# First tokens' norm and first gate/up product inside layer 0's last attention group; a written order behind layer 1's last attention unit

## The chip, the cores and the metric

The kernel runs on one core of one Trainium2 chip. A NeuronCore has five engines that run side by side, each with its own in-order queue: TensorE (PE in the profile) multiplies matrices and also transposes 128x128 blocks against an identity; VectorE (DVE) and ScalarE (ACT) do element-wise work and read results out of PSUM; GpSimd (POOL) does element-wise work in SBUF and issues DMAs; SyncE (SP) issues DMAs. The metric is device time in microseconds (us), lower is better. The kernel before was timed three times.

## The reference

Two transformer blocks are applied to 1024 tokens of width 512, all in float32. Each block is modulated by a condition vector (six columns of `silu(c) @ wmod`: two shifts, two scales and two gates):

```python
h = layernorm(x) * (1 + ca) + sa
x = x + ga * attention(h)
h = layernorm(x) * (1 + cb) + sb
x = x + gb * ffn(h)
```

In layer 0, attention has 32 query heads and 8 key/value heads of width 128 with rotary positions and a causal mask; its weights are 4-bit integers with group scales. Its FFN is `silu(gate(x)) * up(x)` through `down`, hidden width 1376, each of the three matrices with a rank-16 addition. In layer 1, attention has 32 query heads and 8 key/value heads of width 16, with biases. Its FFN is one base matrix, `xf @ base_W.T`, plus a mixture of 28 rank-8 experts, of which the two with the highest logits count, weighted by a softmax over the two.

## The kernel before

The 1024 tokens are eight tiles `x[0]` to `x[7]` of 128 tokens, kept in SBUF. "Half 0" is tiles 0 to 3 and half 1 is tiles 4 to 7. A layer norm works per tile (`bn_stats`, `bn_aggr` on DVE, a square root on ACT, a reciprocal and the scaled copy `xn` on DVE); then a half's four `xn` tiles are transposed chunk by chunk (16 PE transposes of 128x128), and the four chunks are evicted with shift and scale, two by DVE and two by ACT, to `hT`, the transposed input that all products read.

**Layer 0's attention** runs over eight groups (`g`), one for each key/value head with its four query heads, and within a group over eight query tiles in the order 3, 7, 2, 6, 1, 5, 0, 4 (`Step`). A step computes scores, the exponential, the transposition of the probabilities (on DVE, then by DMAs), `context` (probabilities times values, copied by ACT to `ctxT`), `project_o` and `residual`, which multiplies by the gate on DVE and adds to `x[qi]`, before on POOL. Contexts and projections run two to three steps behind the scores. In the last group (`last_group_step`) token tile after token tile becomes final in `x`. The tail behind the loop handles the steps for tiles 5, 0 and 4 (`steps[-3:]`). This whole stage stands under `manual_schedule`: each engine issues the stage's instructions in the order of the program. Outside of such regions a planner orders the instructions of each engine; it may also place later, free instructions among those of a written region.

**Layer 0's FFN** is free. `ln_half` norms and transposes both halves. `merge_gate_up` and `merge_down` add the rank-16 products to the loaded weights (a small matmul into PSUM, then a DVE addition into `gu` or `dwt`). For each of eleven hidden chunks `j` and both halves `b` there are 2x4 matmuls of 128x512 for gate and up, a sigmoid on ACT and two DVE products into `hid`. The weights of chunk 0 (`fw["gu"]`) are loaded and merged during the last attention group; the other chunks' loads go out on SP (`gu`) and POOL (`dwt`) once layer 0's attention frees the memory. `bank()` hands out the seven PSUM banks of the ring.

**Layer 1's attention** runs over sixteen units (`Unit`: query half `Q`, key/value head `g`). Context products run two steps behind; `later` and `tick` keep these due. `normalize` turns a unit's context, divides by the row sums and stores it by four DMAs into `cT`. After the last unit of a query half, `finish` enqueues `project_out` for that half's four tiles, whose result is added to `x` on POOL. From unit 13 on, the order is the planner's.

**Layer 1's FFN**: for half 0 the norm, the products with expert inputs and logits (`ffn1_logits`) and the choice of experts (`ffn1_route`, a chain of some twenty small DVE operations and one ACT exponential) run beside units 13 and 14. `ffn1_turn` weights one tile's expert inputs (`hg`) and transposes them (two PE transposes, two ACT copies to `hgT`); `ffn1_out` makes the base product (4 chunks) and the two expert products in one PSUM bank, applies the gate, adds `x` and stores the tile. Behind the last unit the program has, in this order: the four `ffn1_turn` of half 0, half 1's `project_out`, half 1's norm and transposes, four `ffn1_out` of half 0, then for half 1 the logits, the routing and, tile by tile, `ffn1_turn` and `ffn1_out`.

Of the kernel before, what the change touches and what calls it, by code (L numbers as in the profile page):

```python
# [17 lines left out]
P = 128  # L18
S = 1024
NT = S // P  # L20
D = 512
# [21 lines left out]
def block_kernel(ctx: ExitStack, tc: tile.TileContext, a: dict, out: bass.AP):  # L43
# [120 lines left out]

    keep = ctx.enter_context(tc.tile_pool(name="keep", bufs=1))


    with ExitStack() as st:
# [194 lines left out]

        def residual(u, ps):
            t = tmp("ot")
            nc.vector.tensor_mul(t, ps, mod[0, 2])  # L366
            nc.gpsimd.tensor_tensor(x[u.qi], x[u.qi], t, ALU.add)  # L367

# [229 lines left out]
        for g in range(NKV):  # L598
            for i, qi in enumerate((3, 7, 2, 6, 1, 5, 0, 4)):
# [56 lines left out]
                if old:  # L656
                    residual(old, ps)
        residual(steps[-3], project_o(steps[-3]))
        for old in steps[-2:]:
            context(old)  # L660
            residual(old, project_o(old))

# [4 lines left out]
    big = st.enter_context(tc.tile_pool(name="big", bufs=1))  # L667
    hTc = {}

# [4 lines left out]
    def bank():  # L674
        return sp.tile([P, 512], F32, tag="sc", name="sc")

    xns = {}

# [17 lines left out]
    def ln_turn(half, shift, scale1, chunks=range(NC)):  # L696

        if 0 in chunks:
            hTc[half] = keep.tile([P, NC, 512], F32, tag=f"h{half}", name=f"hT{half}")
        h = hTc[half]  # L700
        for c in chunks:
            ps = bank()
            for i in range(4):
                nc.tensor.transpose(
                    ps[:, bass.ts(i, P)], xns[4 * half + i][:, bass.ts(c, P)], ident
                )
            if c % 2:
                nc.scalar.activation(
                    h[:, c, :], ps, AF.Identity,
                    bias=shift[:, c : c + 1], scale=scale1[:, c : c + 1],  # L710
                )
            else:
                nc.vector.tensor_scalar(
                    h[:, c, :], ps, scale1[:, c : c + 1], shift[:, c : c + 1],
                    ALU.mult, ALU.add,
                )

# [12 lines left out]
    with ExitStack() as f0:  # L730
# [17 lines left out]
        for j in range(NF):  # L748
            nc.gpsimd.dma_start(dwt[:, j, :], a["d_w"][bass.ts(j, P), :])

# [25 lines left out]

        for half in range(2):
            ln_half(half, mod[0, 3], mod[0, 4])

        for pair in range(2):  # L780
            merge_gate_up(1, pair)
        gate_row(0, 5, bank)

        for b in range(2):
            hid[b] = big.tile([P, NF, 512], F32, tag=f"b{b}", name=f"hid{b}")
        for j in range(NF):
            w = gu[:, j] if j else fw["gu"]
            for b in range(2):
                pgu = []
                for m in range(2):  # L790
                    ps = bank()
                    for c in range(NC):
                        nc.tensor.matmul(  # L793
                            ps, lhsT=w[:, m, c, :], rhs=hTc[b][:, c, :],
                            start=(c == 0), stop=(c == NC - 1),
                        )
                    pgu.append(ps)
                sg = wk.tile([P, 512], F32, tag="sg", name="sg")
                nc.scalar.activation(sg, pgu[0], AF.Sigmoid)
                nc.vector.tensor_mul(sg, pgu[0], sg)  # L800
                nc.vector.tensor_mul(hid[b][:, j, :], pgu[1], sg)
            if j in (0, 1, 4, 5):
                merge_gate_up(4 if j < 4 else 8, j % 4)
            elif j in (6, 7, 8):
                for i in range(4 * (j - 6), min(NF, 4 * (j - 5))):
                    merge_down(i)
# [309 lines left out]
    def project_out(t):  # L1116
# [7 lines left out]
        nc.vector.tensor_mul(o, po, mod[1, 2])  # L1124
        nc.gpsimd.tensor_tensor(x[t], x[t], o, ALU.add)

# [82 lines left out]
    def ffn1_turn(t):  # L1209
        lp = late_pool["p"]  # L1210
        hg = lp.tile([P, NE, ER], F32, tag="hg", name="hg")
        nc.vector.tensor_tensor(
# [13 lines left out]

    def ffn1_out(t):
        hgT, eb = late_pool["hgT", t], late_pool["eb"]
        po = bank()
        for c in range(NC):  # L1230
            nc.tensor.matmul(  # L1231
                po, lhsT=tok(c, t), rhs=late_pool["wb"][:, c, :], start=(c == 0), stop=False
            )
        nc.tensor.matmul(po, lhsT=hgT[:, 0, :], rhs=eb[0], start=False, stop=False)
        nc.tensor.matmul(po, lhsT=hgT[: NER - P, 1, :], rhs=eb[1], start=False, stop=True)
        o = tmp("eo")
        nc.vector.tensor_mul(o, po, mod[1, 5])
        nc.vector.tensor_add(o, o, x[t])
        nc.sync.dma_start(out[bass.ts(t, P), :], o)


# [13 lines left out]
    def finish(u):  # L1255
        normalize(u)
        if u.g == NKV - 1:
            for i in range(4):
                later(3 + i, lambda t=4 * u.Q + i: project_out(t))

# [37 lines left out]
    for n, u in enumerate(units):  # L1298
# [29 lines left out]
        while beside and beside[0][0] <= n:  # L1328
            beside.pop(0)[1]()
    for i in range(4):  # L1330
        tick()
        ffn1_turn(i)
    while late:
        tick()
    ln_half(1, mod[1, 3], mod[1, 4])
    for i in range(4):
        ffn1_out(i)
    ffn1_logits(1)
    ffn1_route()
    for t in range(4, NT):  # L1340
        ffn1_turn(t)
        ffn1_out(t)

# [83 lines left out]
```

## Time and profile before

| what | value |
|---|---|
| median of 3 runs | 1906.38 us (1901.47 to 1908.9) |
| the profiled execution's own time | 1906.41 us |
| span in its profile (first to last instruction) | 1903.7 us |
| TensorE (PE) busy | 1816.8 us, 95% of the span |
| VectorE (DVE) busy | 1162.4 us, 61% |
| ScalarE (ACT) busy | 670.2 us, 35% |
| GpSimd (POOL) busy | 483.3 us, 25% |
| mean granted TensorE clock | 0.976 |
| PE busy from 1064.00 to 1118.40 us (end of layer 0's attention to the first gate/up product) | 44.77 of 54.40 us |
| PE busy from 1838.00 to 1899.30 us (half 1's transposes to the last product) | 55.53 of 61.30 us |

The profile is one execution; its times are counted from the start of its span. In a row of the timeline stand the start and the time in us, engine, line of the kernel, operation, output and inputs, shape, the number of instructions and, in brackets, the idle time before it and what ended that. A 128x512 float32 product is recorded as two matmuls. A row of the waits has: who waited for whom, us in total, how often, the longest. "Granted clock" is the share of the full clock that TensorE's throttle let through.

### The profile page before, as it was taken

The page shows a single profiled execution, that of the slowest core. Times are in us where ns is not written, and L with a number is a line of the kernel's source. Part 1 is how long each engine was busy: PE and PEld are TensorE (multiplying, and loading weights), DVE is VectorE, ACT ScalarE, POOL GpSimd, SP SyncE. Part 2 cuts the span into 40 slices and gives each one's busy share as a digit, 9 for nine tenths or more (in the row PEclk, how much of TensorE's full clock was granted, in tenths as well). Part 3 has the DMA queues.
Part 4 walks back from the last instruction along what each step waited for, and adds up shares of the span by engine and source line. Part 5 has one row for each costly group of instructions (what it writes and reads, how often), then busy time and mean ns, then how long its engine had stood idle before and what let it go on. Part 6 is the DMA issues. An engine that isn't in the chain of part 4 may idle for free.

```text
span 1903.7 us, 22550 instructions
## 1 busy us (share of the span) xinstructions
PE 1816.8 (95%) x6578; PEld 847.0 (44%) x6578; DVE 1162.4 (61%) x2820; ACT 670.2 (35%) x1393; POOL 483.3 (25%) x717
## 2 busy tenths in 40 slices
PE   7989999999999999999999989998998989999987
PEld 4444455444454444454444444444543433333434
DVE  5677775777756777756767652323555567677332
ACT  1143433444334344334345410010123433455620
POOL 1234443444424444434444410001001000000010
PEclk9999999999999999999999999999989979999999
DMA  6164552454534544524545450010000011000000
GB/s 224 47 171 119 132 144 73 117 140 125 138 83 108 136 117 122 150 74 108 146 119 142 113 212 1 0 37 14 1 2 8 8 42 37 4 8 8 4 18 33
DMA packets 87034, 156.38 MB, mean 82 GB/s; under 512 B 25264, under 2 KB 33072, under 8 KB 86912
## 3 DMA queue, kind: packets, MB, share of 16 engines
q1 hardware_dynamic: 68480, 114.11, 21.1%
q0 software_dynamic: 18192, 40.42, 8.6%
q8 instruction: 53, 0.87, 0.2%
q14 instruction: 69, 0.57, 0.1%
q10 hardware_dynamic: 240, 0.41, 0.1%
HBM read 74.90 MB, written 2.36 MB: 41 GB/s over the span
## 4 chain that ended last, share of the span: by engine, by line
PE 71%; DVE 15%; issue 5%; ACT 5%; DMA 2%; POOL 1%; SPq 1%; ACTq 0%; POOLq 0%; DVEq 0%
PE mm L347 9%; PE sc L793 8%; PE sc L312 8%; PE mm L200 7%; PE mm L358 7%; PE sc L1043 6%; PE sc L996 5%; PE sc L812 4%; PE ctx L1086 4%; DVE pr L336 3%; PE mm L280 3%; PE sc L893 3%; ACT pr L322 2%; ACT pr L331 2%; PE sc L1231 2%
## 5 line engine op out<-in xcount | busy, mean ns | idle before, releaser
L322 ACT ACTIVATE pr<-sc,nb 128x512 f32<-128x512 f32 (+7 forms) x256 | 189.1, 739 | 508.6 <-DVE nb L320 391.1
L200 PE MATMUL mm<-hT,wf 128*128 128x512 f32 x640 | 294.3, 604 | 10.2 <-DVE t L209 7.3
L338 POOL DMA_DIRECT2D pT<-pr x509 | 251.1, 499 | 146.9 <-DMA pT<-pr 43.1
L312 PE MATMUL sc<-kT,qT 128*128 128x512 f32 (+15 forms) x768 | 263.7, 467 | 3.8 <-ACT pr L322 3.0
L347 PE MATMUL mm<-pT,v 128*128 128x512 f32 x576 | 258.8, 594 | 2.8 <-DVE gu L566 1.6
L336 DVE STREAM_TRANSPOSE pr<-pr 128x512 f32<-128x512 f32 (+7 forms) x256 | 189.2, 760 | 82.4 <-ACT pr L331 78.2
L358 PE MATMUL mm<-wo,ctxT 128*128 128x512 f32 x512 | 230.8, 593 | 3.9 <-ACT ctxT L353 2.8
L1043 PE MATMUL sc<-q,kv 32*128 32x512 f32 (+3 forms) x768 | 214.0, 557 | 8.4 <-DVE mx L1006 8.4
L312 PEld LDWEIGHTS sc<-kT,qT 128*128 128x128 f32 x768 | 141.9, 190 | 159.8 <-issue 144.5
L331 ACT ACTIVATE pr<-pr,rs 128x512 f32<-128x512 f32 (+7 forms) x256 | 190.8, 765 | 8.3 <-DVE rs L329 8.3
L1059 ACT ACTIVATE pspace<-sc 128x512 f32<-128x512 f32 (+3 forms) x303 | 132.1, 495 | 163.4 <-PE sc L1052 125.3
L200 PEld LDWEIGHTS mm<-hT,wf 128*128 128x128 f32 x640 | 120.1, 193 | 149.2 <-issue 122.8
L320 DVE TENSOR_REDUCE nb<-sc 128x1 f32<-128x416 f32 (+31 forms) x256 | 181.1, 707 | 8.8
L996 PE MATMUL sc<-kv,q 32*128 32x512 f32 (+3 forms) x768 | 172.1, 547 | 3.3 <-ACT kv L947 1.4
L367 POOL TENSOR_TENSOR x<-x,ot 128x512 f32<-128x512 f32 x64 | 81.0, 1266 | 349.7 <-DVE ot L366 273.6
L347 PEld LDWEIGHTS mm<-pT,v 128*128 128x128 f32 x576 | 107.6, 190 | 122.2 <-issue 113.0
L1006 DVE CUSTOM_DVE_ANT_0 q<-sc,cwide 128x512 f32<-128x512 f32 (+3 forms) x256 | 125.4, 490 | 56.5 <-PE sc L996 27.2
L793 PE MATMUL sc<-hT,gu 128*128 128x512 f32 x352 | 153.1, 594 | 0.0
L358 PEld LDWEIGHTS mm<-wo,ctxT 128*128 128x128 f32 x512 | 95.9, 190 | 111.4 <-issue 100.9
L1043 PEld LDWEIGHTS sc<-q,kv 32*128 32x128 f32 x768 | 78.0, 192 | 96.6 <-ACT pspace L1059 32.6
L213 POOL TENSOR_TENSOR qT<-t,t 128x512 f32<-128x512 f32 x64 | 86.8, 1356 | 112.1 <-DVE t L209 111.7
L793 PEld LDWEIGHTS sc<-hT,gu 128*128 128x128 f32 x352 | 66.2, 190 | 85.2 <-issue 80.4
(188 smaller groups left out, 1845.6 us busy)
## 6 DMA issues: line engine op xcount, KB each, us to landing
wm<-in_wmodT_dram SPq DMA_DIRECT2D x44, 256.0 KB
wi<-in_qw_q_dram SPq DMA_DIRECT2D x32, 256.0 KB
ws<-in_s_q_dram SPq DMA_DIRECT2D x32, 256.0 KB
wi<-in_qw_o_dram SPq DMA_DIRECT2D x32, 256.0 KB
ws<-in_s_o_dram SPq DMA_DIRECT2D x32, 256.0 KB
pT<-pr SPq DMA_DIRECT2D x64, 128.0 KB
pT<-pr POOLq DMA_DIRECT2D x64, 128.0 KB, 3.2
pT<-pr SPq DMA_DIRECT2D x64, 112.0 KB
```

Source lines behind the costliest of these rows:

```text
L200: nc.tensor.matmul(ps, lhsT=wf[:, c, :], rhs=hT[half][:, c, :], start=(c == 0), stop=(c == NC - 1),)
L312: nc.tensor.matmul(ps[:, n0 : n0 + w], lhsT=q, rhs=kT[u.g][:, n0 : n0 + w], start=True, stop=True)
L320: nc.vector.tensor_reduce(nb, ps[:, : d0 + B], AX.X, ALU.max, negate=True)
L322: nc.scalar.activation(u.pr[:, :, :, s, :].rearrange("p j k i -> p k j i"), ps[:, :nk].rearrange("p (k j i) -> p k j i", j=NB, i=B), AF.Ex ...
L331: nc.scalar.activation(pr, pr, AF.Copy, scale=u.rs[s])
L336: nc.vector.transpose(t, t)
L338: queues[(REP * b + r) % len(queues)].dma_start(u.pT[b * B : (b + 1) * B, r, :, :, :].rearrange("p k s i -> p (k s i)"), t[r * B : (r + 1) ...
L347: nc.tensor.matmul(ps, lhsT=vv[u.g][:, kj, :], rhs=u.pT[:, :, kj, :, :], start=(kj == 0), stop=(kj == u.n - 1),)
L358: nc.tensor.matmul(ps, lhsT=u.ctxT[:, r, :], rhs=wo[u.g][:, r, :], start=(r == 0), stop=(r == REP - 1),)
L793: nc.tensor.matmul(ps, lhsT=w[:, m, c, :], rhs=hTc[b][:, c, :], start=(c == 0), stop=(c == NC - 1),)
L996: nc.tensor.matmul(ps[:, at : at + w], lhsT=u.q[kp, bass.ts(i, P)], rhs=kT1[kp, u.g, n0 : n0 + w], start=True, stop=True,)
L1043: nc.tensor.matmul(ps[:, : QW - q0], lhsT=kT1[kp, u.g, bass.ts(kb, P)], rhs=u.q[kp, q0:QW], start=True, stop=kb < 4 * u.Q,)
```

## The change

Three things are rearranged; the arithmetic stays as it is but for which engine does some additions.

1. In the tail of layer 0's attention, inside the written region, tiles 3, 2 and 1 and then 0 are normed (`ffn_norm`, its `xn` in weight buffers of the attention that are free by then), and half 0's 16 transposes and four evictions stand between `context` and `project_o` of the last step (tile 4). The additions into `x[0]` and `x[4]` move from POOL to DVE.
2. In layer 0's FFN the first gate/up product (chunk 0, half 0) comes first, ahead of half 1's norm (tiles 7, 6, 5, then 4), its transposes and the merges of chunks 1 to 3. The eleven `dwt` loads move from POOL's queue to SP's, behind the `gu` loads.
3. Behind layer 1's last unit all engines follow a written order. Half 1's `project_out` is no longer due from `finish`; it stands behind the first two `ffn1_out`, each tile followed by its norm, with the addition into `x` on DVE. The other two `ffn1_out` stand before and behind half 1's transposes. `ffn1_out` is split into `ffn1_base` and `ffn1_experts`, and in half 1 the letters give the order: b for base, t for turn, e for experts. `hg` gets a second buffer, and each `ffn1_turn` of half 0 stands before a `tick` instead of behind it.

```diff
@@ -163,6 +163,21 @@
     keep = ctx.enter_context(tc.tile_pool(name="keep", bufs=1))
+
+    hTc, xns = {}, {}
+
+    def ln_evict_chunk(h, ps, c, shift, scale1):
+
+        if c % 2:
+            nc.scalar.activation(
+                h[:, c, :], ps, AF.Identity,
+                bias=shift[:, c : c + 1], scale=scale1[:, c : c + 1],
+            )
+        else:
+            nc.vector.tensor_scalar(
+                h[:, c, :], ps, scale1[:, c : c + 1], shift[:, c : c + 1],
+                ALU.mult, ALU.add,
+            )
     with ExitStack() as st:
@@ -361,10 +376,10 @@
                 )
             return ps
-        def residual(u, ps):
+        def residual(u, ps, eng=nc.gpsimd):
             t = tmp("ot")
             nc.vector.tensor_mul(t, ps, mod[0, 2])
-            nc.gpsimd.tensor_tensor(x[u.qi], x[u.qi], t, ALU.add)
+            eng.tensor_tensor(x[u.qi], x[u.qi], t, ALU.add)
         def plan(g, i):
@@ -655,17 +670,46 @@
                     turn_probs(u, b, queues)
                 if old:
                     residual(old, ps)
+
+
+        def ffn_norm(ts, tag, bufs):
+            mv = small.tile([P, 4, 2], F32, tag="mv", name="mv")[:, : len(ts), :]
+            for i, t in enumerate(ts):
+                bs = small.tile([P, 6], F32, tag="bnst", name="bnst")
+                nc.vector.bn_stats(bs, x[t])
+                nc.vector.bn_aggr(mv[:, i, :], bs)
+            rstd = small.tile([P, 4], F32, tag="rstd", name="rstd")[:, : len(ts)]
+            nc.scalar.activation(rstd, mv[:, :, 1], AF.Sqrt, bias=eps_t)
+            nc.vector.reciprocal(rstd, rstd)
+            for i, t in enumerate(ts):
+                xns[t] = wp.tile([P, D], F32, tag=tag, name="xn", bufs=bufs)
+                nc.vector.tensor_scalar(
+                    xns[t], x[t], mv[:, i, 0:1], rstd[:, i : i + 1], ALU.subtract, ALU.mult
+                )
+
         residual(steps[-3], project_o(steps[-3]))
-        for old in steps[-2:]:
-            context(old)
-            residual(old, project_o(old))
+        context(steps[-2])
+        ffn_norm([3, 2, 1], "wi", 3)
+        residual(steps[-2], project_o(steps[-2]), nc.vector)
+        ffn_norm([0], "wf", 2)
+        context(steps[-1])
+        hTc[0] = keep.tile([P, NC, 512], F32, tag="h0", name="hT0")
+        for c0 in range(0, NC, 2):
+            ps = sp.tile([P, 2, 512], F32, tag="sc", name="sc")
+            for c in range(c0, c0 + 2):
+                for t in range(4):
+                    nc.tensor.transpose(
+                        ps[:, c - c0, bass.ts(t, P)], xns[t][:, bass.ts(c, P)], ident
+                    )
+            for c in range(c0, c0 + 2):
+                ln_evict_chunk(hTc[0], ps[:, c - c0, :], c, mod[0, 3], mod[0, 4])
+        residual(steps[-1], project_o(steps[-1]), nc.vector)
     st = ctx.enter_context(ExitStack())
     big = st.enter_context(tc.tile_pool(name="big", bufs=1))
-    hTc = {}
     sp = st.enter_context(tc.tile_pool(name="ring", bufs=7, space=PSUM))
@@ -673,8 +717,6 @@
     def bank():
         return sp.tile([P, 512], F32, tag="sc", name="sc")
-
-    xns = {}
     def ln_tiles(ts):
@@ -704,16 +746,7 @@
                 nc.tensor.transpose(
                     ps[:, bass.ts(i, P)], xns[4 * half + i][:, bass.ts(c, P)], ident
                 )
-            if c % 2:
-                nc.scalar.activation(
-                    h[:, c, :], ps, AF.Identity,
-                    bias=shift[:, c : c + 1], scale=scale1[:, c : c + 1],
-                )
-            else:
-                nc.vector.tensor_scalar(
-                    h[:, c, :], ps, scale1[:, c : c + 1], shift[:, c : c + 1],
-                    ALU.mult, ALU.add,
-                )
+            ln_evict_chunk(h, ps, c, shift, scale1)
     def ln_half(half, shift, scale1):
         ln_tiles(range(4 * half, 4 * half + 4))
@@ -746,7 +779,7 @@
         for j in range(4, NF):
             nc.sync.dma_start(gu[:, j, :, :, :], a["gu_w"][j])
         for j in range(NF):
-            nc.gpsimd.dma_start(dwt[:, j, :], a["d_w"][bass.ts(j, P), :])
+            nc.sync.dma_start(dwt[:, j, :], a["d_w"][bass.ts(j, P), :])
         def merge_gate_up(j0, pair):
@@ -774,31 +807,37 @@
             )
             nc.vector.tensor_tensor(dwt[:, j, :], dwt[:, j, :], ps, ALU.add)
-        for half in range(2):
-            ln_half(half, mod[0, 3], mod[0, 4])
-
+        for b in range(2):
+            hid[b] = big.tile([P, NF, 512], F32, tag=f"b{b}", name=f"hid{b}")
+
+        def gate_up(j, b):
+            w = gu[:, j] if j else fw["gu"]
+            pgu = []
+            for m in range(2):
+                ps = bank()
+                for c in range(NC):
+                    nc.tensor.matmul(
+                        ps, lhsT=w[:, m, c, :], rhs=hTc[b][:, c, :],
+                        start=(c == 0), stop=(c == NC - 1),
+                    )
+                pgu.append(ps)
+            sg = wk.tile([P, 512], F32, tag="sg", name="sg")
+            nc.scalar.activation(sg, pgu[0], AF.Sigmoid)
+            nc.vector.tensor_mul(sg, pgu[0], sg)
+            nc.vector.tensor_mul(hid[b][:, j, :], pgu[1], sg)
+
+
+        gate_up(0, 0)
+        ln_tiles([7, 6, 5])
+        ln_tiles([4])
+        ln_turn(1, mod[0, 3], mod[0, 4])
         for pair in range(2):
             merge_gate_up(1, pair)
         gate_row(0, 5, bank)
-
-        for b in range(2):
-            hid[b] = big.tile([P, NF, 512], F32, tag=f"b{b}", name=f"hid{b}")
         for j in range(NF):
-            w = gu[:, j] if j else fw["gu"]
             for b in range(2):
-                pgu = []
-                for m in range(2):
-                    ps = bank()
-                    for c in range(NC):
-                        nc.tensor.matmul(
-                            ps, lhsT=w[:, m, c, :], rhs=hTc[b][:, c, :],
-                            start=(c == 0), stop=(c == NC - 1),
-                        )
-                    pgu.append(ps)
-                sg = wk.tile([P, 512], F32, tag="sg", name="sg")
-                nc.scalar.activation(sg, pgu[0], AF.Sigmoid)
-                nc.vector.tensor_mul(sg, pgu[0], sg)
-                nc.vector.tensor_mul(hid[b][:, j, :], pgu[1], sg)
+                if (j, b) != (0, 0):
+                    gate_up(j, b)
             if j in (0, 1, 4, 5):
                 merge_gate_up(4 if j < 4 else 8, j % 4)
             elif j in (6, 7, 8):
@@ -1122,7 +1161,7 @@
             )
         o = tmp("ao")
         nc.vector.tensor_mul(o, po, mod[1, 2])
-        nc.gpsimd.tensor_tensor(x[t], x[t], o, ALU.add)
+        (nc.gpsimd if t < 4 else nc.vector).tensor_tensor(x[t], x[t], o, ALU.add)
     late_pool = {}
@@ -1208,7 +1247,7 @@
     def ffn1_turn(t):
         lp = late_pool["p"]
-        hg = lp.tile([P, NE, ER], F32, tag="hg", name="hg")
+        hg = lp.tile([P, NE, ER], F32, tag="hg", name="hg", bufs=2)
         nc.vector.tensor_tensor(
             hg,
             late_pool["ha"][:, t % 4, :NER].rearrange("p (e r) -> p e r", r=ER),
@@ -1224,13 +1263,16 @@
         nc.scalar.copy(hgT[: NER - P, 1, :], ps[: NER - P, P : 2 * P])
         late_pool["hgT", t] = hgT
-    def ffn1_out(t):
-        hgT, eb = late_pool["hgT", t], late_pool["eb"]
+    def ffn1_base(t):
         po = bank()
         for c in range(NC):
             nc.tensor.matmul(
                 po, lhsT=tok(c, t), rhs=late_pool["wb"][:, c, :], start=(c == 0), stop=False
             )
+        late_pool["po", t] = po
+
+    def ffn1_experts(t):
+        hgT, eb, po = late_pool["hgT", t], late_pool["eb"], late_pool["po", t]
         nc.tensor.matmul(po, lhsT=hgT[:, 0, :], rhs=eb[0], start=False, stop=False)
         nc.tensor.matmul(po, lhsT=hgT[: NER - P, 1, :], rhs=eb[1], start=False, stop=True)
         o = tmp("eo")
@@ -1238,6 +1280,10 @@
         nc.vector.tensor_add(o, o, x[t])
         nc.sync.dma_start(out[bass.ts(t, P), :], o)
+    def ffn1_out(t):
+        ffn1_base(t)
+        ffn1_experts(t)
+
     late = []
@@ -1255,8 +1301,8 @@
     def finish(u):
         normalize(u)
         if u.g == NKV - 1:
-            for i in range(4):
-                later(3 + i, lambda t=4 * u.Q + i: project_out(t))
+            for i in range(4 if u.Q == 0 else 0):
+                later(3 + i, lambda t=i: project_out(t))
@@ -1327,19 +1373,28 @@
             open_late()
         while beside and beside[0][0] <= n:
             beside.pop(0)[1]()
+
+
+    end = ExitStack()
+    end.enter_context(tc.manual_schedule())
     for i in range(4):
+        ffn1_turn(i)
         tick()
-        ffn1_turn(i)
     while late:
         tick()
-    ln_half(1, mod[1, 3], mod[1, 4])
-    for i in range(4):
-        ffn1_out(i)
+    for t in (0, 1):
+        ffn1_out(t)
+    for t in range(4, NT):
+        project_out(t)
+        ln_tiles([t])
+    ffn1_out(2)
+    ln_turn(1, mod[1, 3], mod[1, 4])
+    ffn1_out(3)
     ffn1_logits(1)
     ffn1_route()
-    for t in range(4, NT):
-        ffn1_turn(t)
-        ffn1_out(t)
+    for step in "b4 b5 t4 b6 t5 e4 b7 t6 e5 t7 e6 e7".split():
+        {"b": ffn1_base, "t": ffn1_turn, "e": ffn1_experts}[step[0]](int(step[1]))
+    end.close()
 def _layouts(v):
```

## The prediction

> **What bounds the kernel now.** I read the page first: PE is busy 95% of the span and PE carries 71% of the chain that ended last, so time can only come out of PE's own gaps. Then the waits of PE in the two stretches that the change touches (1010 to 1120 us and 1780 to 1904 us):
>
> ```profile
> PE sc L704 <- DVE xn L692: 5.2, 1, 5.2
> ...
> PE sc L1220 <- DVE hg L1212: 6.6, 3, 5.6
> PE sc L704 <- DVE xn L692: 4.4, 1, 4.4
> ```
>
> The transposes (L704) wait for half 1's norm in layer 0's FFN, again in layer 1's, and the turns (L1220) for the routing. PE's timeline at the first place shows what the wait costs on both sides:
>
> ```profile
> 1094.04 4.53 PE L347 MATMUL mm<-pT,v 128*128 128x512 f32 x10
> 1100.00 3.70 PE L358 MATMUL mm<-wo,ctxT 128*128 128x512 f32 x8 [1.43 <-ACT ctxT L353]
> 1104.48 1.96 PE L704 MATMUL sc<-ident,xn 128*128 128x128 f32 x16 [0.79 <-DVE ot L366]
> 1111.67 3.76 PE L704 MATMUL sc<-ident,xn 128*128 128x128 f32 x16 [5.22 <-DVE xn L692]
> 1115.36 2.46 PE L760 MATMUL sc<-lB,lA 16*128 16x384 f32 x16
> ...
> 1118.25 7.03 PE L793 MATMUL sc<-hT,gu 128*128 128x512 f32 x16
> ```
>
> The same 16 transposes take 1.96 us before the idle 5.22 us and 3.76 behind it. The windows tell why: the granted clock is 0.50 from 1111 to 1115 and is back near 1115.5. PE's timeline at the end:
>
> ```profile
> 1817.13 0.43 PE L1086 MATMUL ctx<-pspace,kv 128*32 128x128 f32 x8
> ...
> 1819.80 13.90 PE L1119 MATMUL sc<-wo,cT 128*128 128x512 f32 x32
> 1838.08 3.67 PE L704 MATMUL sc<-ident,xn 128*128 128x128 f32 x16 [4.38 <-DVE xn L692]
> ...
> 1862.60 6.96 PE L1165 MATMUL sc<-wag,hT 128*128 128x252 f32 x32
> 1875.20 0.48 PE L1220 MATMUL sc<-ident,hg 128*128 128x128 f32 x1 [5.64 <-DVE hg L1212]
> ...
> 1875.68 5.74 PE L1231 MATMUL sc<-wb,hT 128*128 128x512 f32 x8
> ...
> 1898.24 1.02 PE L1235 MATMUL sc<-eb,hgT 96*128 96x512 f32 x2
> ```
>
> Two idle gaps, each followed by slow work: transposes at 3.67 instead of 1.96, a base product at 5.74 instead of the 3.60 of the others.
>
> **Change at layer 0's FFN.** Count from the end of the last context, 1098.6, which stays where it is. Is half 0's last norm in time for it? `ctxT` of tile 0 is copied by 1090.4 as before. DVE multiplies tile 5's residual until 1089.7, then norms tiles 3, 2, 1: three statistics at 0.66 with the aggregate, to 1091.7; the square root's table load (1.28) runs 1090.4 to 1091.7 on ACT as before; square root and reciprocal to 1092.4; three `xn` at 0.57 to 1094.1. Tile 0's product ends at 1094.2, as before, so its residual is not delayed: multiply 0.73, add on DVE 0.7 (nearest row: the SBUF addition L1238, 0.69; POOL took 1.27), statistics 0.85, square root 0.35, reciprocal 0.25, `xn` 0.6: ready at 1097.7, 0.9 before PE asks. That square root is now ahead of the `ctxT` copy without waiting, where before the copy stood behind a square root that waited for DVE: the 1.43 us go.
>
> PE then: 16 transposes 1.96 to 1100.6 (cover for the `ctxT` copy, 0.6); `project_o` 3.6 to 1104.1; the ring's first bank still waits for the residual's multiplication (L366), 0.8, to 1104.9; the first gate/up product 6.95 (half of L793's 13.9) to 1111.9. Under it DVE adds `x[4]` (1105.6) and norms it, 2.2, to 1107.8, or 1109.5 if the other three `xn` come first; with a table load for the square root 1110.8: still covered. Transposes at full clock 1.96, merges 2.46, gate transposes 0.6: 1116.9. Before, the same point with one product less was 1118.25. Saved: 1118.25 - (1116.9 - 6.95) = **8.3 us**. From there PE is full until layer 1's preparation, so it stays saved.
>
> At nothing: the `dwt` loads on SP. SP alone moved 371 to 411 GB/s when it loaded `lA`, `lB`, `dA`, `dB` (1099 to 1104), as much as both queues together behind it (397 to 408). Queued behind `gu` on SP, 2.9 MB of `dwt` come last (8.1 MB at 400 GB/s: 20 us), and the first merge into them stands behind chunk 6, seven times 13.9 = 97 us on. `gu` 1 to 3 come sooner than before; without that cover the merges would wait, at most the 7 us in which 2.9 MB pass.
>
> **Change at the end.** Up to the last context (ends 1817.56) nothing changes. In the written order the last `hg` stands on DVE behind `normalize` of the last unit, and the last turn stands on PE ahead of the first base product. So PE waits: context copy on ACT to 1818.3, DVE from 1818.47, `normalize` undisturbed 2.2 (unit 14's rows, 1805.15 to 1807.35), `hg` 0.4, turn 0.3: the first `ffn1_out` starts at 1821.4, with PE idle for some 3.2 us from about 1817.9. Before, `project_out` started at 1819.8. Queued behind that waiting turn is all of PE's rest, and nothing else waits.
>
> From 1821.4 only work that exists now: four `ffn1_out` at 5.15 (1847.14 to 1852.29 and so on) 20.6; `project_out` 13.8; transposes 1.96; logits 6.86; half 1's four tiles at 5.375 (1883.19 to 1888.57) 21.5. Sum 64.7, end at 1886.1 against 1899.26: **13.2 us**. What hides what:
> - `normalize`'s stores are behind 10.3 us of `ffn1_out`.
> - Norms: per tile multiply 0.73, add 0.73, statistics and aggregate 0.9, square root 0.33, reciprocal 0.2, `xn` 0.58, 3.5 us against PE's 3.44. The last `xn` is ready at 1835.2 + 14.0 = 1849.2; the transposes come behind the third `ffn1_out`, at 1850.6. At 4.2 per tile PE would wait 1.4.
> - The evictions lie under the fourth `ffn1_out` (5.15).
> - Routing: from the last logits to the turn now 5.64 + 0.5; two base products give 6.88. Without that cover it costs the 5.6 us plus 2.5 of slow clock of today.
> - The third routed tile's turn and the rest interleave products of 1.7 to 3.4 us with `hg` (0.4) and copies (0.5).
>
> **The clock behind the new gap.** The trace has no gap of 3.2 us. Its nearest rows:
>
> ```profile
> 994.40 4.14 PE L312 MATMUL sc<-kT,qT 128*128 128x512 f32 x6 [2.98 <-ACT pr L322]
> ...
> 1319.69 0.69 PE L704 MATMUL sc<-ident,xn 128*128 128x128 f32 x4 [2.25 <-DVE xn L692]
> 1320.97 8.40 PE L893 MATMUL sc<-wqkv,hT 128*128 128x512 f32 x16 [0.59 <-issue]
> 1332.35 1.10 PE L946 MATMUL sc<-ident,qpad 128*128 128x128 f32 x8 [2.98 <-DVE qpad L919]
> ```
>
> The first was followed by a granted clock of 0.50 from 996 to 999.3 (half of 3.3 us lost, 1.65), the second by 0.50 from 1320 to 1326 (8.40 where the same products later take 5.4, 3.0 lost), the third by 1.00. The longer gaps of 4.38 and 5.64 lost 2.1 and 2.5. Ends 0 and 3.0; I take 1.65, from the row whose gap and neighbours are nearest. The end is then worth 11.5. The Trainium skill ("TensorE: Matmul & The Clock Gate", "HAM oscillation — how this bites in real kernels") states that gaps up to about 3.4 us do no harm; by that rule the term is 0 and the time 1885.0, but the row at 991.4 disagrees.
>
> Sum: 1906.4 - 8.3 - 11.5 = **1886.6**. The profiled execution (1906.41, span plus 2.7) equals the median of 1906.38, so nothing is converted.
>
> **Rivals.**
> - *Norms behind the product.* If the planner queues tiles 7 to 4's norms on DVE behind the first product's own multiplications, they start at 1112.6: three statistics, square root and `xn` 4.5, tile 4's 2.2, transposes at 1119.3 instead of 1111.9, plus 1.8 of slow clock. Layer 0 then loses 0.9 (7.4 + 1.8 - 8.3) and the time is 1895.8. For: program order. Against: in this trace the planner put free statistics (1096.32) ahead of the written multiplication at 1103.73.
> - *Transposes count as idle for the clock.* Behind the first product come 5.0 us of transposes, 16-row merges and transposes. If they let the clock fall, the next product loses what the row at 1320.97 lost, 3.0: 1889.6. For: that row, where 1.5 us of transposes stand ahead of the gap. Against: behind the 5.22 us gap the clock came back during the transposes themselves. The Trainium skill (same page, "Part 4: PE-mode transpose") states that transposes do not count as busy; the row at 1320.97 fits that, those 3.8 us from 1111.67 to 1115.5 contradict it.
> - *No change or slower.* Units 13 to 15 are planned freely and the region behind them is now chained. If the planner then puts context products ahead of exponentials that ACT has not done, PE waits at each as at 1805.17 (0.82). There are 24 key blocks, each with two bunches of products. One wait per block costs 19.7: 1906.3. Two per block cost 39.4: 1926. It ends over 0.5% slower from 1.2 us a block. For: ACT is 93% busy at 1776 to 1786. Against: the contexts run two blocks behind, and before the change only two such waits stand in the trace (1.6 in all).
> - *The change doesn't order what it says*, if something of the region is held by a buffer (six `tmp` slots, of which four hold `xn`): one stored tile's chain, 1.4 us of DVE plus some 3 to land, per wait: 1891.
>
> **Numbers.** Forecast 0.70; norms behind the product 0.07; transposes as idle 0.10; buffers 0.05; no change 0.04, slower 0.04. The range takes in no clock loss (1885.0), the ring's bank free at once (0.8 less) and planner luck of 2 to 3 us below, 1881; above, the clock at 3.0, a late last norm, and the norm rival, 1896. About 0.5% (9.5 us) is what a measurement of this kernel can tell from no change: faster means under 1896.9, slower over 1915.9. Forecast and the first three small rivals are faster (0.92), less 0.04 for two of them together: faster 0.88, same 0.08, slower 0.04.
>
> **What would show it.** Right: no L692 wait of PE over 1 us left at either place; the product's 16 matmuls (now `gate_up`) directly behind the last `project_o`; one gap of about 3 us before the first base product, the only one until the end; granted clock 1.00 from the routing on. Wrong: transposes of half 1 in layer 0 starting over 2 us behind the first product; PE waiting for `hg` behind the second base product; context waits in units 13 to 15 summing to over 5 us.

## The result: 22 us faster, and the profile after

The changed kernel takes 1884.56 us (median of 4 runs, 1882.88 to 1886.94) against 1906.99 us (4 runs, 1901.47 to 1908.9). The ratio is 0.9888 with a 95% interval from 0.9865 to 0.9911. The forecast was 1886.6 us with a range from 1881 to 1896. The profiled execution of the changed kernel took 1886.94 us, with a span of 1885.1. It is the slowest of its four runs, so the two spans differ by 18.6 us and the medians by 22.4. Only one execution below, the profiled one of experiment 2's first run, was of another kind (2642.33 us at a mean granted clock of 0.69), and no comparison uses it.

PE's timeline at the end of layer 0's attention, to be held against the one before (columns as there):

```profile
1095.07 4.45 PE L362 MATMUL mm<-pT,v 128*128 128x512 f32 x10
1099.46 1.94 PE L701 MATMUL sc<-ident,xn 128*128 128x128 f32 x16
1101.23 3.60 PE L373 MATMUL mm<-wo,ctxT 128*128 128x512 f32 x8
1105.71 7.10 PE L819 MATMUL sc<-hT,gu 128*128 128x512 f32 x16 [0.88 <-DVE ot L381]
1112.65 1.91 PE L746 MATMUL sc<-ident,xn 128*128 128x128 f32 x16
1114.49 2.46 PE L793 MATMUL sc<-lB,lA 16*128 16x384 f32 x16
1116.89 0.66 PE L154 MATMUL sc<-ident,spread 128*128 128x128 f32 x4
1117.38 7.03 PE L819 MATMUL sc<-hT,gu 128*128 128x512 f32 x16
```

The gap of 5.22 us is gone, and with it the slow transposes: both sets take 1.9 us. The one wait left is for the ring's first bank. The stage now starts a microsecond later in the span (1099.52 for 1098.57), so it is measured from the end of the last context.

PE's timeline at the end of the kernel:

```profile
1808.09 0.43 PE L1125 MATMUL ctx<-pspace,kv 128*32 128x128 f32 x8
...
1811.81 0.33 PE L1259 MATMUL sc<-ident,hg 128*128 128x128 f32 x1 [2.93 <-DVE hg L1251]
...
1812.09 3.60 PE L1269 MATMUL sc<-wb,hT 128*128 128x512 f32 x8
...
1841.28 1.91 PE L746 MATMUL sc<-ident,xn 128*128 128x128 f32 x16
...
1854.98 7.03 PE L1269 MATMUL sc<-wb,hT 128*128 128x512 f32 x16
1861.85 0.27 PE L1259 MATMUL sc<-ident,hg 128*128 128x128 f32 x1
...
1874.80 0.33 PE L1259 MATMUL sc<-ident,hg 128*128 128x128 f32 x1 [1.81 <-DVE hg L1251]
...
1875.07 1.90 PE L1276 MATMUL sc<-eb,hgT 128*128 128x512 f32 x2
1876.77 1.88 PE L1277 MATMUL sc<-eb,hgT 96*128 96x512 f32 x2
```

The waits of 4.38 us for the norm and 5.64 us for the routing are gone: the transposes at 1841.28 and the first routed turn at 1861.85 start without any. The first gap was forecast (3.2 us, it is 2.93). The second, 1.81 us with expert products at 1.90 instead of 1.02 behind it, was not.

Where the 18.6 us come from, by stretches of PE's timeline (ends of the records; "net" is less 6.95 us for the product that is already done):

| stretch | before | after | difference |
|---|---|---|---|
| A: end of layer 0's last context to the first product behind the gate transposes, net | 19.68 | 10.91 | -8.77 |
| middle: from there to layer 1's last context, with the 6.95 us | 699.31 | 698.09 | -1.22 |
| B: end of layer 1's last context to the last product | 81.70 | 71.85 | -9.85 |
| start of the span to A, and the last stores | 1103.01 | 1104.25 | +1.24 |

### The profile page after: what moved, and what is told of

Read it like the earlier page. It is cut to its first block, busy times and chain, and to the rows that moved or that the text cites. A ratio compares the mean times of both kernels' runs of the same rounds, so it can differ in the third digit from the quotient of the medians.

```text
span 1885.1 us, 22551 instructions
## 1 busy us (share of the span) xinstructions
PE 1810.6 (96%) x6578; PEld 844.4 (45%) x6578; DVE 1169.5 (62%) x2831; ACT 671.7 (36%) x1398; POOL 469.5 (25%) x700
## 4 chain that ended last, share of the span: by engine, by line
PE 72%; DVE 15%; ACT 5%; issue 4%; DMA 2%; SPq 1%; POOL 1%; ACTq 0%; DVEq 0%; POOLq 0%
PE mm L362 10%; PE sc L819 8%; PE sc L327 8%; PE mm L215 7%; PE mm L373 7%; PE sc L1082 6%; PE sc L1035 5%; PE sc L851 4%; PE ctx L1125 4%; DVE pr L351 3%; PE mm L295 3%; PE sc L932 3%; ACT pr L337 2%; ACT pr L346 2%; DVE t L224 2%
```

## The experiments

Each run gives A and B from its own profile in the same way; that separates terms of 2 us, which the total times, 4 to 7 us apart between runs of one kernel, can't. Where no number of runs is given, it is one execution. The kernel before was timed beside them again: its median was 1906.75 us beside experiments 1 to 4 (9 runs, 1901.95 to 1908.42) and 1900.63 beside experiments 9 to 11 and the second run of experiment 2 (7 runs, 1898.73 to 1906.63).

**1. Only the layer 0 part.** The end is as before, the rest as in the changed kernel.

```diff
-    end.enter_context(tc.manual_schedule())
-    for i in range(4):
-        ffn1_turn(i)
-        tick()
...
+    for i in range(4):
+        tick()
+        ffn1_turn(i)
...
```

> Only the layer 0 part of the change; the end stays as before. Theory (the two parts are independent, each saves only what lies in its own stretch): from the end of the last context of layer 0's attention to the first product behind the gate transposes, 17.9 us with one product (6.95) already inside, that is 10.9 net against 19.7 before; the end stretch, from the last context to the last product, stays at 81.7. Time 8.8 below before: about 1898. Rival (the parts lean on each other, or the planner lays the free stages between them differently): the stretch between them changes by over 2 us, and the time lies outside 1895 to 1901.

Measured: A 10.90, B 81.66, and 1895.84 us (6 runs), ratio 0.9949 [0.9935, 0.9964]. A and B are what they are in the changed kernel and in the kernel before, so the parts are independent. The middle was 694.0 instead of 698 or 699, over 2 us away, which the rival had named as one of its two signs; the last section shows that this is the clock's.

**2. Only the end.** Layer 0 as before. It ran twice: the first run gives the time, the second the stretches.

```diff
-        residual(steps[-2], project_o(steps[-2]), nc.vector)
-        ffn_norm([0], "wf", 2)
...
+        for old in steps[-2:]:
+            context(old)
+            residual(old, project_o(old))
```

> Only the end of the change (written order, split products, additions on DVE); layer 0 as before. Theory: end stretch 71.9 us as in the changed kernel, with PE's two gaps of 2.9 and 1.8 us, layer 0 stretch 19.7 as before; time 9.9 below before, about 1897. Rival (the end gains part of its 9.9 us only because everything arrives earlier or in another memory layout): end stretch over 74 us.

> Only the end of the change, once more, for its stretches: the profiled execution of the second experiment ran at a mean granted clock of 0.69. Theory: end stretch 71.9 us, or 70.1 where the clock does not fall behind the gap of 1.8 us; layer 0 stretch 19.7. Rival: end stretch over 74 us.

Measured: 1898.27 us, ratio 0.9955 [0.9937, 0.9973] over three executions; in the second run A 19.77 and B 73.55. That second run took 1900.65 us in all, no less than the kernel before beside it (1900.63), although its B is 8.2 us shorter than that of the kernel before (81.70): its middle, 700.0 us, is the longest of all. B lies between what the two theories named: it is 1.7 above the changed kernel's 71.85. PE's timeline of that run shows the same two gaps, and slow products behind both:

```profile
1823.70 0.33 PE L1220 MATMUL sc<-ident,hg 128*128 128x128 f32 x1 [2.93 <-DVE hg L1212]
...
1823.97 5.29 PE L1230 MATMUL sc<-wb,hT 128*128 128x512 f32 x8
...
1888.38 0.33 PE L1220 MATMUL sc<-ident,hg 128*128 128x128 f32 x1 [1.81 <-DVE hg L1212]
...
1889.94 1.91 PE L1238 MATMUL sc<-eb,hgT 96*128 96x512 f32 x2
```

The product at 1823.97 took 5.29 where the changed kernel's took 3.60: 1.69 us, the whole difference. So the clock term that the prediction put behind the first gap exists, but it fell out in one execution and not in the other.

**3. The two turns moved.** Half 0's last turn ahead of the last unit's `normalize`, tile 7's ahead of tile 5's experts.

```diff
     for i in range(4):
         ffn1_turn(i)
-        tick()
+        if i != 2:
+            tick()
...
-    for step in "b4 b5 t4 b6 t5 e4 b7 t6 e5 t7 e6 e7".split():
+    for step in "b4 b5 t4 b6 t5 e4 b7 t6 t7 e5 e6 e7".split():
```

> The changed kernel with two moves in the written order: the last turn of half 0 ahead of the last unit's normalize, and the turn of tile 7 ahead of the experts of tile 5. Theory (both gaps of PE in the end come from DVE's own queue: a weighting that could run is queued behind operations that wait): the gap of 2.9 us goes, the gap of 1.8 us goes and with it the half clock behind it (1.7 us); end stretch 71.9 - 3.1 - 3.5 = 65.2 us, time about 1878. Rival (the next thing is late in their place: the base product waits for the copies of the turns, or the last experts for the copy of tile 7's turn, or the clock falls anyway): end stretch 68 us or more.

Measured: B 64.97, 1875.72 us (4 runs, 1872.33 to 1877.89), ratio to before 0.9839 [0.9822, 0.9857]. Both gaps are gone; no wait of PE is left in B:

```profile
1800.74 0.33 PE L1259 MATMUL sc<-ident,hg 128*128 128x128 f32 x1
...
1801.02 0.27 PE L1259 MATMUL sc<-ident,hg 128*128 128x128 f32 x1
...
1801.24 3.60 PE L1269 MATMUL sc<-wb,hT 128*128 128x512 f32 x8
...
1860.25 0.27 PE L1259 MATMUL sc<-ident,hg 128*128 128x128 f32 x1
...
1860.47 1.02 PE L1276 MATMUL sc<-eb,hgT 128*128 128x512 f32 x2
```

Its median is the lowest of this study; by B, experiments 5 and 9 are its equals.

**4. The first product back at its old place.** Half 0's early norm stays.

```diff
-        gate_up(0, 0)
         ln_tiles([7, 6, 5])
```

> The changed kernel with the first gate/up product back at its old place behind the gate transposes; half 0's early norm and transposes stay. Theory (the product is the cover for tile 4's norm): PE waits about 3.6 us from the last projection to the last xn of half 1, the transposes behind that gap run at half clock (1.8 us more); layer 0 stretch 15.4 us net against 10.9, so the early norm alone is worth 4.3 of the 8.8 us and the product's place 4.5. Without a clock drop 13.6. Rival (the early norm does it all, and the cover is not needed because the planner fills the wait with merges): 10.9 to 11.5.

Measured: A 15.35.

```profile
1101.18 3.60 PE L373 MATMUL mm<-wo,ctxT 128*128 128x512 f32 x8
1108.43 2.93 PE L746 MATMUL sc<-ident,xn 128*128 128x128 f32 x16 [3.66 <-DVE xn L734]
```

PE waits 3.66 us for tile 4's norm, and the transposes and merges behind are slow. So 4.4 of the 8.8 us hang on the product as a cover (wait and clock).

**5. The end without the written region.** Same program order, planned by the scheduler.

```diff
-    end.enter_context(tc.manual_schedule())
```

> The changed kernel without the written region at the end: the same program order, but the planner orders each engine. Theory (the gain of the end is in the split products and the program order, and both gaps are made by the written queues): the planner puts the weightings where they can run, both gaps go, end stretch 65 to 68 us against 71.9. Rival (the written order carries the gain): the planner lets the base products of half 1 start late or packs the routing without cover, and the end stretch is 75 us or more.

Measured: B 64.98, in one execution of 1877.76 us. DVE's timeline shows what the planner does otherwise:

```profile
1804.98 0.39 DVE L1251 TENSOR_TENSOR hg<-ha,oh 128x224 f32<-128x224 f32 x1 [9.45 <-PE sc L1260]
1805.92 0.39 DVE L1251 TENSOR_TENSOR hg<-ha,oh 128x224 f32<-128x224 f32 x1 [0.55 <-PE sc L1260]
1807.00 0.71 DVE L1141 STREAM_TRANSPOSE q<-q 128x512 f32<-128x512 f32 x1 [0.69 <-ACT q L1134]
```

Both `hg` (the lines with L1251) stand ahead of `normalize` (L1141). In the changed kernel the second of them stands behind it:

```profile
1810.77 0.71 DVE L1148 STREAM_TRANSPOSE q<-q 128x512 f32<-128x512 f32 x1
1811.40 0.35 DVE L1251 TENSOR_TENSOR hg<-ha,oh 128x224 f32<-128x224 f32 x1
```

The gain of the end thus needs no written region: it lies in what this version keeps, the split products, the additions on DVE, the second `hg` buffer and the program order, which no run takes apart. The written region as it was changed gave 6.9 us of it back, and a planned order ends where that of experiment 3 does.

**6. Only tile 7's turn moved.**

> The changed kernel with only the turn of tile 7 moved ahead of the experts of tile 5. Theory: the second gap (1.8 us) and the slow experts behind it (1.7 us) go, the first gap of 2.9 us stays without a clock drop: end stretch 68.4 us. Rival (the half clock is owed to the first gap or to the moment, not to the second gap): the experts of tiles 6 and 7 still take 1.9 us a piece, 70 us.

Measured: B 68.12; the experts behind take 1.02, the gap of 2.93 stays, with a base product of 3.60 behind it. Together with experiment 3, the first gap is worth 68.12 - 64.97 = 3.15 us, the second 71.85 - 68.12 = 3.73.

**7. The `dwt` loads back on POOL's queue.**

```diff
-            nc.sync.dma_start(dwt[:, j, :], a["d_w"][bass.ts(j, P), :])
+            nc.gpsimd.dma_start(dwt[:, j, :], a["d_w"][bass.ts(j, P), :])
```

> The changed kernel with the down weights' loads back on POOL's queue. Theory: nothing moves, as the first merges have their weights in time either way: layer 0 stretch 10.9 us net, plus or minus 0.3. Rival (two queues share the DMA engines, and the gate and up weights of chunks 1 to 3 then come too late for the merges, which now stand earlier): DVE waits for loads ahead of its first merge, up to 7 us.

Measured: A 13.12, so the rival was right. DVE's timeline:

```profile
1117.08 3.80 DVE L798 TENSOR_TENSOR gu<-gu,sc 128x384 f32<-128x384 f32 x8 [2.67 <-DMA gu<-in_gu_w_dram]
```

The first merge waits 2.67 us for the `gu` loads, and PE 1.9 us behind it for a bank. The DMA engines are full (a share of 1.01 to 1.03 from 1108 to 1118), and with both queues at work they carry `dwt` beside `gu`. In the kernel before the first merge (1116.31) waited for no load. This queue move looks like a detail and is 2.2 of the 8.8 us. It is worth more than A shows: behind PE's wait the granted clock is 0.50 from 1119.7 to 1123.1, and the first product of the middle takes 8.73 us where the changed kernel's takes 7.03.

**8. Half 1's projections ahead of the first two output tiles.**

```diff
-    for t in (0, 1):
-        ffn1_out(t)
     for t in range(4, NT):
         project_out(t)
         ln_tiles([t])
+    for t in (0, 1):
+        ffn1_out(t)
```

> The changed kernel with half 1's projections ahead of the first two output tiles of half 0. Theory: the stores of the last unit are the only thing that the two tiles covered; they are issued from about 1811.5 on this trace's clock and are needed 2.6 us behind the first product (the last chunk of tile 4), so PE waits 0 to 1.5 us; the norms get more cover, not less: end stretch 71.9 to 73.4 us. Rival (the stores land late, 4 us or more, as with loads of that queue): PE waits over 3 us there and the clock falls: 76 us.

Measured: B 70.98, below what either theory named. PE stood still for 0.58 us ahead of the seventh projection matmul. The profile names no releaser for it ("issue"), but experiment 10 waits for the stores at the same place, and in both that matmul starts 6.89 us behind the last context. The second gap, however, passed without a fall of the clock:

```profile
1872.13 0.33 PE L1259 MATMUL sc<-ident,hg 128*128 128x128 f32 x1 [1.81 <-DVE hg L1251]
...
1872.41 1.02 PE L1276 MATMUL sc<-eb,hgT 128*128 128x512 f32 x2
```

The same 1.81 us, between the same instructions as in the changed kernel, and experts at 1.02 instead of 1.90.

**9. Another PSUM bank for the last projection**, on top of experiment 3.

```diff
-        residual(steps[-1], project_o(steps[-1]), nc.vector)
+        ps = sp.tile([P, 2, 512], F32, tag="sc", name="sc")[:, 0, :]
...
+        residual(steps[-1], ps, nc.vector)
```

> The two moves of the third experiment, and the last projection of layer 0's attention writes into a score bank, so that the ring's first bank, which the first gate/up product takes, no longer waits for the last residual's multiplication. Theory: PE's wait of 0.9 us ahead of that product goes: layer 0 stretch 10.0 us net against 10.9; end stretch 65.0 as in the third experiment; time about 1875. Rival (the ring waits for the whole old pool, whichever bank was read last): 10.9 again.

Measured: A 10.91, with the wait of 0.88 for the residual's multiplication as before; B 64.98; 1877.43 us (4 runs), ratio 0.9872 [0.9846, 0.9898] to the 1900.63 us beside it. The bank that was read last is not the reason, or not by itself. Whether the ring waits for the whole old pool or happens to begin at the new bank stays open.

**10. Projections first, with the turns moved** (experiments 3 and 8 together).

> The two moves of the third experiment, and half 1's projections ahead of the first two output tiles. Theory (the first two output tiles cover the last unit's stores once the gap ahead of them is closed): the stores were usable 6.9 us behind the last context with the gap; without it the projections start 0.4 us behind the last context and need them 2.6 us later, so PE waits 3.9 us more, and the clock may fall: end stretch 68.9 to 70.6 us against 65.0. Rival (the stores land earlier too, or the planner's order inside a tile hides them): 65 to 66.

Measured: B 70.64.

```profile
1813.95 13.09 PE L1158 MATMUL sc<-wo,cT 128*128 128x512 f32 x26 [3.73 <-DMA cT<-q]
```

PE waits 3.73 us for the last unit's stores, and the products behind take 13.09 us where 26 at 0.43 make 11.2. The two output tiles are the stores' cover; behind the gap of 2.93 us (experiment 8) only 0.58 us of it showed.

**11. The two additions into `x` back on POOL.**

> The changed kernel with the last two additions into x in layer 0's tail back on POOL. Theory: tile 0's xn comes 0.55 us later (1.27 for 0.69 us) and PE had 0.1 us to spare, so the transposes and the last projection start 0.5 us later; tile 4's stays covered by the first product: layer 0 stretch 11.4 us net against 10.9. Rival (the additions were the reason for the gain): 13 us or more.

Measured: A 11.59, with PE waiting 0.63 us for tile 0's `xn`. The engine change is worth 0.7 us.

## Why the prediction was right, step by step

- **The norm of tile 0 in time.** Right by less than forecast: `xn` was ready at 1099.32 and PE asked at 1099.46, 0.14 us to spare for 0.9. DVE's timeline shows two statistics of half 1 (L727), which the planner put into the written region, ahead of tile 0's aggregate and reciprocal:

```profile
1096.72 0.69 DVE L679 BATCH_NORM_STATS2 bnst<-x 128x6 f32<-128x512 f32 x1
1097.33 0.68 DVE L727 BATCH_NORM_STATS2 bnst<-x 128x6 f32<-128x512 f32 x1
1097.92 0.17 DVE L680 BATCH_NORM_AGGREGATE mv<-bnst 128x2 f32<-128x6 f32 x1
1098.01 0.66 DVE L727 BATCH_NORM_STATS2 bnst<-x 128x6 f32<-128x512 f32 x1
...
1098.80 0.52 DVE L686 TENSOR_SCALAR xn<-x,mv,rstd 128x512 f32<-128x512 f32 x1
```

- **Stretch A, 8.3 forecast, 8.8 measured.** Bank wait 0.88 for 0.8. The half microsecond is in the sum of records: neighbouring records overlap by 0.06 to 0.17 us, 0.7 us in all from the last context to the product behind the gate transposes, and the forecast added most of them end to end.
- **"At nothing: the `dwt` loads."** The sum was right to add nothing, and the reason beside it was right: `gu` comes sooner, and without that the merges would wait. But the heading makes the move look idle, and experiment 7 puts it at 2.2 us of the 8.8. SP's bandwidth alone was not the question; the share that POOL's loads took was.
- **The first gap, 3.2 us.** Right: 2.93, and the first base product starts 3.57 us behind the last context (3.84 forecast).
- **The clock behind it, 1.65 us.** The row was real but not certain. Among the seven profiles with this gap, the product behind it was slow in two (experiment 4 and the second run of experiment 2: 4.78 and 5.29 for 3.60) and at full speed in five. Neither 1.65 nor the 0 that the prediction weighs beside it holds as a fixed term; the last section says what the traces show of it.
- **The gap that was not forecast.** "The third routed tile's turn and the rest interleave products of 1.7 to 3.4 us with `hg` (0.4) and copies (0.5)." This step failed. In the written order tile 7's `hg` stands on DVE behind tile 5's two output operations, which wait for tile 5's experts on PE; and on PE the turn comes directly behind those experts. DVE's timeline of the changed kernel:

```profile
1873.02 0.69 DVE L1279 TENSOR_TENSOR eo<-sc,gate 128x512 f32<-128x512 f32 x1 [3.65 <-PE sc L1277]
1873.75 0.69 DVE L1280 TENSOR_TENSOR eo<-eo,x 128x512 f32<-128x512 f32 x1
1874.36 0.38 DVE L1251 TENSOR_TENSOR hg<-ha,oh 128x224 f32<-128x224 f32 x1
```

  0.69 + 0.69 + 0.38 us and the handovers are the 1.81 us. Tile 6's turn has the same queue ahead of it, but a base product of 3.44 us between. The prediction walked DVE's queue at the first turn and only listed durations here. It cost 1.81 + 1.75 of slow experts; the loss forecast at the first gap, 1.65, did not come. The first gap was 0.3 us shorter than forecast. So B saved 9.85 for 11.5. That it missed by no more, and that the profiled time of 1886.94 us lies 0.3 us from the forecast, is partly luck: 3.6 us that were not forecast stand against 1.65 that did not come, and the middle is 1.2 us shorter, its loss to the clock being less.
- **The signs set down for being right.** The first three came in the main: no wait for `xn` is left, the product stands directly behind the last `project_o` (but for the forecast wait for its bank), and a gap of about 3 us stands ahead of the first base product. But that gap is not the only one until the end, and the granted clock is 1.00 from the routing on only until 1875.1, where the second gap's slow piece begins.
- **The norms of half 1.** Right: the last `xn` at 1839.8, PE asks at 1841.28, 1.5 us to spare (1.4 forecast).
- **Rivals.** Norms behind the product: the planner put the statistics ahead, as in the trace of before. Transposes as idle: behind the first product the granted clock stayed 1.00 from 1110 to 1122, through 1.9 us of transposes and 2.5 of merges. For these float32 transposes that speaks against what the Trainium skill says ("TensorE: Matmul & The Clock Gate", "Part 4: PE-mode transpose"), that transposes do not count as busy, but weakly, since 1.9 us are few; the 3.8 us of transposes in the kernel before, at whose end the clock came back, are the stronger row. Units 13 to 15: PE's waits for context copies are two, 1.6 us in all, as before. Buffers: none.

## What to carry to other kernels

In a written order, walk each engine's queue past every instruction that waits, not only the first of a repeated pattern: a small operation that could run, queued behind operations that wait (`normalize` at the first gap, tile 5's output at the second), made both gaps here, and moving two turns was worth 6.9 us. Before writing an order, run the same program order under the planner; here it found by itself what the hand-made order missed. And measure such edits by stretches of the timeline, because the total carries several microseconds of clock that have nothing to do with the edit.

## What the runs showed of the hardware

The middle stretch holds nearly the same work in all profiles, yet it took 692.6 to 700.0 us. Summing (1 - granted clock) over it in steps of 2 us gives the time lost to the throttle:

| run | middle | lost to the clock | rest |
|---|---|---|---|
| before | 699.3 | 30.7 | 668.6 |
| after | 698.1 | 29.0 | 669.1 |
| experiment 1 | 694.0 | 23.9 | 670.1 |
| experiment 3 | 692.6 | 22.2 | 670.4 |
| experiment 2, second run | 700.0 | 30.7 | 669.3 |

In all thirteen profiles with this stretch the rest is 668.6 to 670.5, so the spread between runs there is mostly the clock's. The thirteen losses take only five values, 22.2, 23.9, 25.6, 29.0 and 30.7 us, and these lie 1.7 us or twice that apart: the loss comes in pieces of 1.7 us. The length of a gap doesn't decide it: 2.93 us let the clock fall in two of seven profiles, 1.81 us in four of six. A half-clock piece lasted 3.4 us (1875.1 to 1878.5 in the changed kernel), which costs half of that:

```profile
1874.00:1875.00 1.00, 0.20 (x2) 0.21 (x3) 0.74 (x2) 0.00 (x0) 0.00 (x0) 1.00 0.00 0
1875.00:1876.00 1.00, 1.00 (x4) 0.48 (x3) 0.00 (x0) 0.43 (x2) 0.00 (x0) 0.54 0.65 256
1876.00:1877.00 1.00, 1.00 (x3) 0.48 (x2) 0.00 (x0) 0.00 (x0) 0.00 (x0) 0.50 0.02 6
1877.00:1878.00 1.00, 1.00 (x2) 0.44 (x2) 0.00 (x0) 0.00 (x0) 0.00 (x0) 0.50 0.00 0
1878.00:1879.00 1.00, 1.00 (x3) 0.28 (x2) 0.31 (x1) 0.00 (x0) 0.00 (x0) 0.76 0.00 0
```

(Windows of the changed kernel: the stretch and its length, the busy time of PE, weight loads, DVE, ACT and POOL, then the granted clock, the DMA share and GB/s.) The Trainium skill ("TensorE: Matmul & The Clock Gate", "What's actually happening") states that the gate looks at activity in windows of about 3.4 us that run freely, whatever the kernel does. The length of the slow piece agrees.

The traces' own records of the granted clock go further. In all fourteen, every half-clock piece that ends before the trace does lasts 3.41 us or a whole multiple of it, and all changes of the clock within one trace lie on one grid of 3.41 us (to 0.005 us). The grid stands elsewhere against the program in every run. Laid over the two gaps of the end, it sorts all thirteen cases: the clock fell where one grid piece held 1.81 us of PE's idle time or more (2.88, 2.37 and four times 1.81), and it held where the gap was so divided between two pieces that neither had more than 1.74 (1.74, 1.62, 1.61, 1.59, 1.57, 1.56 and 1.29). So where a gap falls on the grid accounts for equal gaps that end differently. All thirteen cases bear that out, but no run moved a gap on purpose, and 1.81 us is no limit for other places: 1.01 us of idle at 1441.5 in the kernel before and 1.37 us at 1116.3 in experiment 7 were followed by half clock too. For a sum it means: the clock term behind each of these two gaps is 0 or up to 1.7 us and can't be known ahead, because the program doesn't set the grid. Other gaps cost more; the prediction's row at 1319.69 lost 3.0 us behind 2.25.
